# A convolution, Fourier and feed-forward kernel whose instruction order comes from a planner: other priorities, other slacks, and a charge for the tiles of 64

## The chip, the core and the metric

The kernel runs on one core of one Trainium2 chip. The metric is device microseconds (us) from the start of an execution to its end. The kernel before took 4438.63 us (the median of three runs, 4436.33 to 4449.61 us). One further execution was recorded by the hardware profiler, and that one took 4424.09 us.

## What is computed

The input is 32 images of 56 x 56 pixels with 96 channels. Cut to what matters, the reference does this to each image (all in float32 unless said otherwise):

```
layer 0   rw = sigmoid(mean(x) @ Wr + br)                  4 weights of experts for an image
          h  = relu(bn1(x @ (rw . Wpw)))                   96 -> 384 channels
          h  = relu(bn2(depthwise 3x3 with rw . Wdw))      384 channels
          x  = bn3(h @ (rw . Wpwl)) + x                    384 -> 96
layer 1   n  = layernorm(x) over channels, on 3136 tokens
          h  = relu(bn(n @ w1.T))                          96 -> 192
          X  = fft(h) over the tokens; relu of a diagonal complex product; y = real(ifft)
          x  = x + bn(y @ w2.T)                            192 -> 96
          n  = layernorm(x)
          x  = x + W2 . relu(W1 . n + b1) + b2             operands rounded to fp8 (5 exponent bits),
                                                           96 -> 384 -> 96
```

## The kernel before, in words

**The stages.** Images go through a software pipeline; three images are in work at a time. For image b the stages, with the name of the PSUM tile by which the profile knows them (the profile leaves buffer numbers out, so ps_w1 and ps_w2 are both "ps_w"), are:

- *expansion* (L678): ps_pw, 96 to 384 channels, in two halves p = 0 and 1 of the image; ScalarE evacuates to the padded tiles hp (`expanded`, L698).
- *depthwise convolution*. Part of it is on TensorE (`convolved_tensor`, L713): nine taps as diagonal 32 x 32 products, 16 array tiles at a time. One "block" of it is 144 products in the program, 288 matmuls in the profile (a float32 product runs as two). There are three blocks for an image: two in the first half (i = 0 and 1) and one in the second; below they are the first, second and third block, ps_dw. The rest is on VectorE (`convolved_vector`, L757), eight steps of scalar_tensor_tensor for a set of columns, written to the tiles h2 ("h" in the profile).
- *projection* (L783): ps_pwl, 384 to 96, four strips s = 0 to 3; VectorE adds the shortcut into x.
- *forward* (L863), two streams by the parity of s: for each strip transposes (ps_t_a) for the moments of the norm, a small product with `spread` into the same tile, then for each group of four rows of the Fourier grid ps_w1 (tiles of 96 x 64: eight products), VectorE's four `ha`, ps_a (tiles of 64 x 64: eight products), ScalarE's `g`, and a DMA to the DRAM tile gd.
- *frequency loads* (L930): when all of image b's gd is written, the first group of frequencies (16) is loaded into the one tile g2; when TensorE has read that tile, the second group (13) is loaded into the same tile.
- *frequencies* (L944): ps_b, three kinds for each group, then the complex nonlinearity on ScalarE, VectorE and GpSimd (`nonlinearity` L963, `imaginary_parts` L1001), then `spectrum` (L1019): ps_w2, ScalarE's zo, ps_c, VectorE, DMA to the DRAM tile yd.
- *inverse* (L1064), two streams by parity: loads of a strip of x1 and of yd (tile yt), ps_d, VectorE adds, transposes ps_t_f, the norm, ps_n, and the feed-forward ps_f1 (three chunks, `hidden` L1150: ScalarE, VectorE, GpSimd) and ps_f2, then GpSimd's add and the store of the output.

Work on image 16 in layer 0 stands in the program beside forward of 15 and 16, frequencies of 15 and inverse of 14. All DMAs of the steady state are issued by SyncE, in program order.

**PSUM.** There are four tiles of two banks, tag "ps", taken in turn. A TensorE group that takes a tile therefore waits until the evacuation of the group four takings earlier is done; a depthwise block takes two.

**What sets the order.** Nothing is scheduled by hand. Every stage is a generator ("stream") that yields the engine its next step runs on, the events it needs and the buffers it takes. `Plan.run` (L206) keeps a model clock for each engine; `tick` (L162) adds a modelled cost when an instruction is issued; `run` picks among the streams that could go on the one with the smallest (earliest start, priority, ready):

```
at = max(ready, self.free[stream.engine] + self.SLACK[stream.engine])
key = (at, stream.priority, ready)
```

The start is thus the later of "inputs ready" and "engine free plus SLACK" (L147, one number for each engine), and among streams that could all start when the engine is free the lower priority number wins. `mm` (L580) charges a product by its size, divided by `share` where several array tiles run at once; the depthwise block has a fixed extra of 0.4 us (L739). The order so chosen is the order of every engine's program; the chip then runs it with semaphores, and a wrong model costs waits, not errors.

**Fillers.** When the planner sees TensorE idle between two groups, `psum` (L326) puts products of the constant dftb_s into the new tile ahead of the work (L330), one for each 0.19 us of expected idle time over 0.3 us, at most 40. They compute nothing that is used. The program before holds 794.

Of the kernel before, what the change touches and what calls it, by code (L numbers as in the profile page):

```python
# [111 lines left out]
PE, DVE, ACT, POOL, SP = "PE", "DVE", "ACT", "POOL", "SP"  # L112
# [21 lines left out]
class Plan:  # L134
# [9 lines left out]

    MARGIN = 1.07

    SLACK = {PE: 0.05, DVE: 0.3, ACT: 0.05, POOL: 1.2, SP: 0.0}  # L147

    def __init__(self, **buffers):
        self.free = dict.fromkeys((PE, DVE, ACT, POOL, SP), 0.0)  # L150
# [144 lines left out]
def kernel(  # L295
# [311 lines left out]
    def mixing():  # L607

        for b in range(NB):
            yield ACT, [("x", b)] + [("x1", b - 2, s) for s in range(NS) if b >= 2]  # L610
            pooled = mixp.tile([C, 1], F32, tag="pooled", name=f"pooled_{b}")
            A.activation(xs[b], xs[b], AF.Copy, accum_out=pooled)
            yield DVE
            pool_b = mixp.tile([C, 128], F32, tag="pool_b", name=f"pool_b_{b}", bufs=1)
            V.tensor_scalar(pool_b, ones, pooled, 1.0 / N, ALU.mult, ALU.mult)
            rw = mixp.tile([128, NE + 1], F32, tag="rw", name=f"rw_{b}")
            yield POOL
            P.memset(rw[:, NE : NE + 1], 1.0)
            yield PE, (), 1
            ps = psum(f"ps_rw_{b}")  # L620
            mm(ps[:, 0:NE], pool_b, wr_s)
            yield DVE
            V.tensor_add(rw[:, 0:NE], ps[:, 0:NE], br_s)
            plan.release()
            yield ACT
            A.activation(rw[:, 0:NE], rw[:, 0:NE], AF.Sigmoid)
            yield DVE
            wk = mixp.tile([C, M], F32, tag="wk", name=f"wk_{b}")
            V.tensor_scalar_mul(wk, wpw_s[:, 0, :], rw[:C, 0:1])
            for e in range(1, NE):  # L630
                W.behind.scalar_tensor_tensor(wk, wpw_s[:, e, :], rw[:C, e : e + 1], wk, ALU.mult, ALU.add)
            yield DVE
            by = rw.rearrange("p (k e) -> p k e", k=1)
            prod = mixp.tile([128, NMIX, NE + 1], F32, tag="prod", name=f"prod_{b}", bufs=1)
            W.tensor_mul(prod, stk_s, by.to_broadcast([128, NMIX, NE + 1]))
            small = mixp.tile([128, NMIX], F32, tag="small", name=f"small_{b}")
            V.behind.tensor_reduce(small, prod, AX.X, ALU.add)
            mixed[b] = wk
            small_of[b] = small
            plan.done("wk", b)  # L640
            for c in range(NPE):
                plan.spawn("diagonals", 7, diagonals(b, c))
            yield DVE
            wk2 = mixp.tile([128, NC3, C], F32, tag="wk2", name=f"wk2_{b}")
            V.tensor_scalar_mul(wk2, wpwl_s[:, 0], rw[:, 0:1])
            for e in range(1, NE):
                W.behind.scalar_tensor_tensor(wk2, wpwl_s[:, e], rw[:, e : e + 1], wk2, ALU.mult, ALU.add)
            yield SP

            wk2s[b] = [wk2]  # L650
            for q in range(1, G):
                wk2q = mixp.tile([128, NPE, C], F32, tag=f"wk2_{q}", name=f"wk2_{b}_{q}")
                for to, at in turned(q):
                    Q.dma_start(wk2q[to], wk2[at, 0:NPE])
                wk2s[b].append(wk2q)
            arrives(4 * 3 * 128 * NPE * C, "wk2", b)
# [56 lines left out]
    def convolved_tensor():  # L713

        for b, p, before in parts_of_all():
            for i, wave in enumerate(WAVES[p]):
                needs = [("prj", *before)] if before else []
                for c in {c for c, _ in wave}:
                    needs += [("hp", b, p, c, 0), ("hp", b, p, c, 1), ("diag", b, c)]
                yield PE, needs, 2  # L720
                ps = [psum(f"ps_dw_{b}_{p}_{i}_{u}") for u in range(2)]
                for t in range(9):
                    w, h = divmod(t, 3)
                    for q, (c, k) in enumerate(wave):
                        for g in range(G):
                            at = slice(32 * g, 32 * g + 32)
                            to = 32 * ((g + q) % G)
                            bank = 512 * (q % 2)
                            lo = BW * (k % G) + w
                            mm(  # L730
                                ps[q // 2][to : to + 32, bank : bank + TB],
                                diag[b % 2][c][at, t, :],
                                hp[c][at, lo : lo + BW, h : h + S],
                                start=(t == 0),
                                stop=(t == 8),
                                share=12.7,
                            )

                plan.tick(PE, 0.4)  # L739
                plan.done("dwt", b, p, i)  # L740
                plan.spawn("evac dw", 1, convolved(b, p, i, wave, ps))

    def convolved(b, p, i, wave, ps):
        for q, (c, k) in enumerate(wave):
# [118 lines left out]
    def forward(parity):  # L863


        for b in range(NB):
            for s in range(parity, NS, 2):
# [7 lines left out]
                for q0 in range(0, n, 4):  # L875
                    yield PE, (), 1
                    ps = psum(f"ps_w1_{b}_{s}_{q0}")
                    for q in range(4):
                        for r in range(2):

                            at = S + PB * (lo + q0 + q) + S * r - 8
                            mm(
                                ps[SP64 * r : SP64 * r + SP64, 256 * q : 256 * q + CH],
                                xpad[b % 2][:, at : at + SP64],
                                w1c,
                                share=2,
                            )
                    if q0 + 4 == n:
                        plan.done("x read", b, s)
                    yield DVE  # L890
# [14 lines left out]
                    for q in range(0, 4, 2):  # L905
                        for odd in range(2):
                            for r in range(2):
                                c = r ^ odd
                                at = slice(SP64 * r, SP64 * r + SP64)
                                to = 512 * odd + 128 * q  # L910
                                mm(
                                    ps[SP64 * c : SP64 * c + SP64, to : to + CH],
                                    dfta_s[at, lo + q0 + q + odd, :],
                                    ha[at, q + odd, :],
                                    share=3.3,
                                )
                    yield ACT
                    g = sp.tile([128, 4, CH], F32, tag=f"g{parity}", name=f"g_{b}_{s}_{q0}")
                    A.copy(
# [24 lines left out]
    def frequencies():  # L944


        n = 0
        flat = g2.rearrange("p k m -> p (k m)")
        for b in range(NB):
            for i, (k0, nk) in enumerate(GROUPS):  # L950
                for kind in range(NKIND):
                    yield PE, [("g2 here", n)] + [("z read", n - 1)] * (n >= 1 and kind == 2), 1
                    ps = psum(f"ps_b_{b}_{k0}_{kind}")
                    size = (nk + (kind < 2)) // 2
                    for j in range(size):
                        at = 2 * CH * j + 128 * kind
                        mm(ps[:, 128 * j : 128 * j + PB], flat[:, at : at + 128], dftb_s)
                    plan.spawn("nonlinearity", 3, nonlinearity(n, b, k0, size, kind, ps))
                plan.done("g2", n)
                plan.spawn("spectrum", 3, spectrum(n, b, i, k0, nk))  # L960
                n += 1

    def nonlinearity(n, b, k0, nk, kind, ps):  # L963
# [12 lines left out]
        if k0 == 0 and kind < 2:  # L976
# [3 lines left out]
            V.tensor_add(u[:n0, 0, 0:1], u[:n0, 0, 0:1], dc[:n0, kind, 0:1])  # L980
            V.tensor_add(w[:n0, 0, 0:1], w[:n0, 0, 0:1], dc[:n0, kind, 1:2])
            yield ACT
            plan.spawn("imaginary parts", 5, imaginary)
        else:
            plan.spawn("imaginary parts", 2, imaginary)
            A.activation(u, re, AF.Identity, scale=rd, bias=rb)


# [75 lines left out]
    def inverse(parity):  # L1064


        for b in range(NB):
            for s in range(parity, NS, 2):
# [47 lines left out]
                for c in range(NC3):  # L1116
                    yield PE, (), 1
                    ps = psum(f"ps_f1_{b}_{s}_{c}")
                    for j in range(2):
# [2 lines left out]
                            fw1[:, 128 * c : 128 * c + 128],  # L1122
                            n[:, j * TH : j * TH + TH],
                        )
                    plan.spawn("hidden", 1, hidden(parity, b, s, c, ps, h8))
                yield PE, [("h8", b, s, c) for c in range(NC3)], 1
                ps = psum(f"ps_f2_{b}_{s}")
                for c in range(NC3):
# [34 lines left out]

    with tc.manual_schedule():
        for name, priority, stream in (
            ("loads", 2, loads()), ("mixing", 5, mixing()), ("inverse", 6, inverse(0)),
            ("inverse", 0, inverse(1)), ("frequency loads", 4, frequency_loads()),
            ("frequencies", 6, frequencies()), ("forward", 0, forward(0)),
            ("forward", 1, forward(1)), ("projection", 8, projection()),
            ("vector", 6, convolved_vector()), ("tensor", 2, convolved_tensor()),  # L1170
            ("expansion", 9, expansion()),
        ):
            plan.spawn(name, priority, stream)
        plan.run()
# [114 lines left out]
```

## Time and profile before

| What | Value |
|---|---|
| median of three runs | 4438.63 us |
| the profiled execution, its own time | 4424.09 us |
| its span, first to last instruction | 4422.3 us |
| busy: TensorE matmul, VectorE, ScalarE, GpSimd | 94%, 77%, 61%, 22% |
| granted TensorE clock, mean | 0.994 |
| first block ps_dw of image 0 starts at | 64.5 us |
| first block ps_dw of image 31 starts at | 4136.1 us |
| from one image's first block to the next one's, images 4 to 26 | 133.7 us on average |

The profiled execution was 14.5 us faster than the median of the runs. "PE" is TensorE's matmuls, "PEld" its weight loads, "DVE" VectorE, "ACT" ScalarE, "POOL" GpSimd, "SP" SyncE. In a view of waits a line reads: the engine and the tile that waited, the instruction that ended the wait, us in total, how often, the longest. "issue" is a wait that ended with no semaphore that the profile shows. In a timeline a line reads: start, duration, engine, source line, operation, tiles, shape, count, and in brackets the idle time before it and what ended it. The source line L291 is the helper that records instructions of VectorE, ScalarE, GpSimd and SyncE, and L587 is the helper that records products, so rows are told apart by their tiles.

### The profile page before, as it was taken

How to read it: one execution, taken by the hardware profiler on the slowest of the kernel's cores; microseconds unless marked ns; L12 is line 12 of the kernel's file. 1: busy time of each engine (PE TensorE's matmuls, PEld its weight loads, DVE VectorE, ACT ScalarE, POOL GpSimd, SP SyncE). 2: the span in 40 equal slices, each digit the busy share in tenths (PEclk: the TensorE clock that was granted, in tenths of full speed). 3: DMA queues.
4: the chain of work that ended last, by engine and by line, in shares of the span. 5: the costliest groups of instructions: out<-in, count | busy, mean ns of one | idle time of the engine just before them, and what ended most of it. 6: DMA issues, size and time to landing. Idle time of an engine off the chain costs nothing.

```text
span 4422.3 us, 121145 instructions
## 1 busy us (share of the span) xinstructions
PE 4160.7 (94%) x51578; PEld 2841.8 (64%) x51578; DVE 3385.6 (77%) x7256; ACT 2697.5 (61%) x4360; POOL 968.2 (22%) x1015
## 2 busy tenths in 40 slices
PE   6999999999999999999999999999999999999999
PEld 4666666666666566666666666666666666665678
DVE  6777877777878778777778887778777778787774
ACT  3465566665676666676655675655666656665565
POOL 2012222212222212222112222122222122222123
PEclk9999999999999999999999999999999999999999
DMA  3333343433344333344333434332434333444342
GB/s 87 85 93 101 78 114 95 104 94 90 91 108 105 98 96 89 96 102 108 99 98 79 106 98 109 93 103 75 114 95 107 91 97 89 104 105 100 81 107 60
DMA packets 336048, 424.96 MB, mean 96 GB/s; under 512 B 134928, under 2 KB 254544, under 8 KB 332208
## 3 DMA queue, kind: packets, MB, share of 16 engines
q1 hardware_dynamic: 333172, 417.00, 37.1%
q8 instruction: 406, 6.65, 0.7%
q14 instruction: 134, 1.10, 0.1%
q10 hardware_dynamic: 2336, 0.20, 0.0%
HBM read 202.60 MB, written 205.06 MB: 92 GB/s over the span
## 4 chain that ended last, share of the span: by engine, by line
PE 78%; DVE 7%; DMA 6%; ACT 5%; issue 3%; SPq 1%; ACTq 0%; POOL 0%; POOLq 0%; DVEq 0%
PE ps_dw L587 20%; PE ps_w L587 11%; PE ps_pw L587 10%; PE ps_pwl L587 9%; PE ps_b L587 6%; PE ps_f L587 5%; PE ps_c L587 3%; DMA yt<-yd 3%; PE ps_d L587 3%; PE ps_a L587 3%; ACT h L291 3%; PE ps_t_f L591 2%; DMA yd<-zo 2%; DVE ha L291 2%; PE ps_pw L330 1%
## 5 line engine op out<-in xcount | busy, mean ns | idle before, releaser
L291 DVE SCALAR_TENSOR_TENSOR h<-hp,small,h 128x1792 f32<-128x1792 f32 (+2 forms) x768 | 1315.0, 1712 | 20.5 <-ACT h L291 7.6
L587 PE MATMUL ps_dw<-hp,diag 32*32 32x448 f32 x27648 | 886.0, 552 | 70.0 <-issue 69.4
L587 PEld LDWEIGHTS ps_dw<-hp,diag 32*32 32x32 f32 x27648 | 531.3, 103 | 360.9 <-issue 194.1
L291 POOL CAST h<-h 128x784 fp8e5<-128x784 f16 x384 | 367.3, 970 | 1431.5 <-DVE h L291 1431.5
L587 PE MATMUL ps_pw<-x,wk 96*128 96x448 f32 (+1 forms) x1344 | 585.4, 568 | 19.8 <-ACT yt L291 19.8
L291 ACT ACTIVATE h<-ps_dw,small 128x448 f32<-128x448 f32 x384 | 225.2, 633 | 617.5 <-PE ps_dw L587 617.5
L587 PE MATMUL ps_pwl<-h,wk 128*96 128x448 f32 x1344 | 525.8, 539 | 0.0
L291 ACT ACTIVATE nl<-ps_b,nl_s 128x448 f32<-128x448 f32 (+2 forms) x576 | 347.4, 661 | 150.2 <-PE ps_b L587 86.9
L291 ACT ACTIVATE hp<-ps_pw,small 128x896 f32<-128x896 f32 (+2 forms) x384 | 355.9, 956 | 121.2 <-PE ps_pw L587 121.1
L291 POOL TENSOR_TENSOR x<-x,y 96x784 f32<-96x784 f32 x128 | 291.4, 2277 | 582.1 <-DVE y L291 578.5
L291 POOL TENSOR_TENSOR nl<-nl,nl 128x448 f32<-128x448 f32 (+1 forms) x192 | 221.9, 1156 | 757.1 <-ACT nl L291 743.0
L291 DVE SCALAR_TENSOR_TENSOR ha<-ps_w,rstd_a,nshift 128x192 f32<-128x192 f32 x896 | 307.9, 407 | 94.1 <-PE ps_w L587 93.8
L587 PEld LDWEIGHTS ps_pwl<-h,wk 128*96 128x96 f32 x1344 | 216.4, 163 | 252.2 <-issue 242.3
L587 PEld LDWEIGHTS ps_pw<-x,wk 96*128 96x128 f32 x1344 | 238.0, 190 | 210.7 <-issue 169.2
L587 PEld LDWEIGHTS ps_w<-w_s,z 128*112 128x112 f32 (+1 forms) x2816 | 351.5, 177 | 26.7 <-issue 20.5
L587 PE MATMUL ps_w<-w_s,z 128*112 128x96 f32 (+2 forms) x2816 | 367.0, 284 | 0.0
L291 ACT ACTIVATE nt<-yt,nm,rstd_f 112x96 fp8e5<-112x96 f32 x896 | 334.2, 454 | 41.3 <-DVE nm L291 41.3
L587 PE MATMUL ps_b<-dftb_s,g 112*128 112x112 f32 x2816 | 351.8, 277 | 7.4 <-DMA g<-gd 4.6
L587 PEld LDWEIGHTS ps_b<-dftb_s,g 112*128 112x128 f32 x2816 | 335.5, 193 | 27.8 <-ACT h L291 10.4
L587 PE MATMUL ps_w<-w1c,x 96*64 96x192 f32 x3584 | 334.0, 332 | 7.7 <-ACT h L291 7.0
L291 DVE TENSOR_SCALAR h<-h,fb 128x784 f16<-128x784 f16 x384 | 229.9, 613 | 140.4 <-ACT h L291 137.9
L291 ACT CAST h<-ps_f 128x784 f16<-128x784 f32 x384 | 294.4, 822 | 49.1 <-PE ps_f L587 44.7
(163 smaller groups left out, 5737.3 us busy)
## 6 DMA issues: line engine op xcount, KB each, us to landing
gd<-g SPq DMA_DIRECT2D x448, 192.0 KB
g<-gd SPq DMA_DIRECT2D x64, 672.0 KB
x<-in_x_dram SPq DMA_DIRECT2D x32, 1176.0 KB
x<-x SPq DMA_DIRECT2D x128, 294.0 KB
yt<-yd SPq DMA_DIRECT2D x128, 294.0 KB
out_dram<-x SPq DMA_DIRECT2D x128, 294.0 KB
g<-gd SPq DMA_DIRECT2D x64, 546.0 KB
x<-x SPq DMA_DIRECT2D x96, 336.0 KB
```

What stands on the lines that cost most here:

```text
L291: return getattr(self.namespace, name)(out, *args, **kw)
L330: nc.tensor.matmul(ps[:PB, 0:PB], dftb_s, dftb_s, start=True, stop=True)
L587: nc.tensor.matmul(to, lhsT, rhs, start=start, stop=stop)
L591: nc.tensor.transpose(to, ap, eye)
```

## The change

The operations of the computation stay what they are. Changed are the numbers by which the planner orders them: two engines' slacks, the priorities of most streams, and two new charges on the model clock of TensorE, 0.1 us after each group of ps_w1 and 0.16 us after each group of ps_a.

```diff
-    SLACK = {PE: 0.05, DVE: 0.3, ACT: 0.05, POOL: 1.2, SP: 0.0}
+    SLACK = {PE: 0.05, DVE: 0.2, ACT: 0.1, POOL: 1.2, SP: 0.0}
...
-                plan.spawn("diagonals", 7, diagonals(b, c))
+                plan.spawn("diagonals", 6, diagonals(b, c))
...
-                plan.spawn("evac dw", 1, convolved(b, p, i, wave, ps))
+                plan.spawn("evac dw", 5, convolved(b, p, i, wave, ps))
...
                                 share=2,
                             )
+                    plan.tick(PE, 0.1)
                     if q0 + 4 == n:
                         plan.done("x read", b, s)
                     yield DVE
...
                                     share=3.3,
                                 )
+                    plan.tick(PE, 0.16)
                     yield ACT
...
-                    plan.spawn("nonlinearity", 3, nonlinearity(n, b, k0, size, kind, ps))
+                    plan.spawn("nonlinearity", 2, nonlinearity(n, b, k0, size, kind, ps))
...
-            plan.spawn("imaginary parts", 5, imaginary)
+            plan.spawn("imaginary parts", 3, imaginary)
         else:
-            plan.spawn("imaginary parts", 2, imaginary)
+            plan.spawn("imaginary parts", 4, imaginary)
...
-                    plan.spawn("hidden", 1, hidden(parity, b, s, c, ps, h8))
+                    plan.spawn("hidden", 0, hidden(parity, b, s, c, ps, h8))
...
-            ("loads", 2, loads()), ("mixing", 5, mixing()), ("inverse", 6, inverse(0)),
-            ("inverse", 0, inverse(1)), ("frequency loads", 4, frequency_loads()),
-            ("frequencies", 6, frequencies()), ("forward", 0, forward(0)),
-            ("forward", 1, forward(1)), ("projection", 8, projection()),
-            ("vector", 6, convolved_vector()), ("tensor", 2, convolved_tensor()),
+            ("loads", 6, loads()), ("mixing", 1, mixing()), ("inverse", 3, inverse(0)),
+            ("inverse", 7, inverse(1)), ("frequency loads", 1, frequency_loads()),
+            ("frequencies", 7, frequencies()), ("forward", 5, forward(0)),
+            ("forward", 3, forward(1)), ("projection", 9, projection()),
+            ("vector", 8, convolved_vector()), ("tensor", 6, convolved_tensor()),
             ("expansion", 9, expansion()),
```

Both programs were built and their orders laid side by side. From about the fourth image on each repeats one pattern for every image. This is TensorE's pattern in the part of an image around the third depthwise block, in the numbers of image 16 (names are tile, image, then strip, group or chunk):

```
before  ... pw_16_1_1_1, pwl_16_1, t_a_16_0 spread, d_14_3, t_a_16_1, n_14_0, b_15_0_0, t_f_14_3,
        w1_16_0_0, t_a_16_1 spread, f1_14_0_0, f1_14_0_1, a_16_0_0, f1_14_0_2, b_15_0_1, w1_16_0_4,
        w1_16_1_0, a_16_0_4, n_14_3, a_16_1_0, f2_14_0, f1_14_3_0..2, w1_16_1_4, b_15_0_2,
        dw_16_1 (third block), f2_14_3, a_16_1_4, w2_15_0_0, b_15_16_0, c_15_0_0, ...
after   ... pw_16_1_1_1, pwl_16_1, d_14_2, t_a_16_0 spread, b_15_0_0, n_14_1, t_a_16_1, t_f_14_2,
        f1_14_1_0, f1_14_1_1, t_a_16_1 spread, f1_14_1_2, b_15_0_1,
        dw_16_1 (third block), w1_16_1_0, n_14_2, w1_16_0_0, f1_14_2_0..2, a_16_1_0, f2_14_1,
        a_16_0_0, b_15_0_2, w1_16_1_4, f2_14_2, w1_16_0_4, a_16_1_4, fillers, w2_15_0_0, a_16_0_4,
        b_15_16_0, c_15_0_0, d_14_3, ...
```

In both programs SyncE's second load of g2 waits for b_15_0_2, and ps_b of the second group (b_15_16_0) waits for that load. The program after holds 752 fillers, 42 fewer; all other counts of products are the same.

## The prediction

> **What bounds the kernel now.** I read the page first, then TensorE's waits, then the timelines of TensorE and SyncE around the costliest one.
>
> ```profile
> span 4422.3 us, 121145 instructions
> PE 4160.7 (94%) x51578; PEld 2841.8 (64%) x51578; DVE 3385.6 (77%) x7256; ACT 2697.5 (61%) x4360; POOL 968.2 (22%) x1015
> q8 instruction: 406, 6.65, 0.7%
> ```
>
> TensorE is busy 94% of the span, so it is the bound; the other three have room. What the order can change is TensorE's idle time, 262 us, of which 37 us is one wait before the first image. The view of TensorE's waits splits the rest (us in total, times, longest):
>
> ```profile
> PE ps_dw L587 <- issue: 69.4, 38, 3.9
> PE ps_a L587 <- DVE ha L291: 24.2, 29, 0.8
> PE ps_d L587 <- DMA yt<-yd: 23.0, 23, 1.9
> PE ps_pw L587 <- ACT yt L291: 19.8, 30, 0.7
> PE ps_t_f L591 <- DVE x L291: 18.6, 30, 0.7
> PE ps_a L587 <- ACT h L291: 12.8, 30, 0.4
> PE ps_n L587 <- DVE nl L291: 12.2, 29, 0.4
> ```
>
> All but the first and third come 29 or 30 times, once an image: they are places in the repeating order. The largest is inside the depthwise block, and no semaphore ended it. TensorE's timeline of one image (start, duration), then SyncE's, then the DMA view of 2071.3 to 2078.8 us and of 2078.8 to 2081 us:
>
> ```profile
> 2069.71 2.04 PE L587 MATMUL ps_b<-dftb_s,g 112*128 112x112 f32 x16
> 2071.68 6.89 PE L587 MATMUL ps_dw<-hp,diag 32*32 32x448 f32 x224
> 2081.73 2.13 PE L587 MATMUL ps_dw<-hp,diag 32*32 32x448 f32 x64 [3.16 <-issue]
> ```
> ```profile
> 2071.33 0.87 SPq L291 DMA_DIRECT2D g<-gd  x2
> ```
> ```profile
> q1 hardware_dynamic: 1455, 1.10, 78.1%
> ```
> ```profile
> q1 hardware_dynamic: 29, 0.01, 4.5%
> q8 instruction: 1, 0.02, 3.9%
> ```
>
> The third block begins at 2071.68, just after b_15_0_2 has freed g2 and SyncE has issued the second load of g2 (2071.33). While that load runs (its packets span 2072.3 to 2079.2) the queue of instructions moves nothing; its packet starts at 2078.9, as the load ends, and TensorE goes on at 2081.7. 406 packets for 51578 matmuls are one for 127 matmuls. A block starts a matmul every 29 ns and uses 127 in 3.7 us, half the load's 7 us. From first to last start an undisturbed block takes 8.3 us. By that measure (it counts the pipeline's last half us, which the waits leave out) the 32 third blocks lose 94.5 us, the first blocks 13.7 and the second ones 1.3.
>
> [...] 6.65 MB in 406 packets, 254 weight loads and matmuls each. [...] here the instruction packet came only when the load ended. [...] beyond the usual step from start to start, a change costs 0.25 us out of tiles of 64 (ps_w1, ps_a), 0.45 us out of 32, 0.09 us out of the rest.
>
> **The change part by part.** *TensorE's own work.* Counted in the built orders, the products are the same, so their time (counts by the trace's steps from start to start) stays. Passages out of tiles of 64 rise from 354 to 379: 25 x 0.25 = +6 us. Fillers fall from 794 to 752: 42 x 0.2 = -8 us at most, less where they covered idle time. Passages and fillers counted in, both orders come to 125.0 us an image in the repeating part, and an image takes 133.7. The charge of the model buys nothing by itself; what counts is what becomes of the 8.7 us of waits.
>
> *The third block moves ahead of b_15_0_2*: it starts 57 us into an image's work instead of 72, and the load that stalled it is triggered 9 us after its end. During the load's 8 us TensorE then runs ps_w1, ps_f2, ps_a and ps_w2, some 130 matmuls in 9.5 us. In the block above 131 matmuls ran between the point where the packet was due (127 after the last one) and the stall, so the instructions in hand last the load out. Around its new place SyncE has only two stores of x1 and six small copies of wk2. I take the loss of the third blocks from 94.5 to 5 us: **-90**. Bounds: 0 and -94.5.
>
> *The first block* lost 13.7 us beside the loads of x1 and yt, issued 1 to 2 us after its start. They now stand about 3 us earlier: **-5**, between -13 and +10.
>
> *Waits outside the blocks*, from start to start (the view above leaves out the pipeline's end, so these are larger). Before they come to 6.05 us an image over 27 images: ps_a behind ha 1.15, ps_d behind yt 0.94, ps_pw behind yt 0.86, ps_t_f behind x 0.79, ps_a behind h 0.50, ps_n behind ha 0.49, a filler behind h 0.40, ps_w1 behind h 0.30, eight small ones 0.62. For both orders I measured each wait's lead: the TensorE work between the group that feeds an evacuation and the group that waits. Where the lead is short of the evacuations queued plus about 0.3 us for the semaphores (ps_pw: lead 0.20, yt 0.72, waited 0.86) the rest is the wait.
> - Gone: ps_w1 to ps_a had leads of 1.2 and 1.3 against four ha of 0.41; it now has 2.0 or more. ps_pw behind yt, ps_n behind ha and ps_w1 behind h go with their neighbours. A filler stays at 0.4, ps_a behind h at 0.35, ps_t_f (leads 3.0 to 4.5 where they were 2.8 to 3.3) at 0.5.
> - ps_d behind yt: the chain is x's load (6.2 us), gd's writes, g2's load (landed 11.7 us after x's), then yt. It passes one store of x1 (1.6 us) that stood before it, but the first of these ps_d stands 1.4 us earlier. I take 0.5.
> - New: f1_14_0_2 behind ha_15_2_4 (lead 1.55, need 1.7) 0.4. In the stretch b_15_0_0 to b_15_0_1 ScalarE has seven evacuations of 0.6 to 0.8 us for PSUM queued (nl, n8, yt, h16): f1_14_1_0 0.7, f1_14_1_1 (lead 0.34 behind yt) 1.1, b_15_0_1 0.6, and the spread product of t_a_16_1 (lead 1.31, VectorE's statistics 2.7, of which 1.8 have then been waited) 0.1. That of t_a_16_2 (lead 2.26) 0.7. w2_15_0_0 behind z 0.25. x of strip 1, now behind wk2 (1.6 us) on VectorE: 0.3. The second load of g2 (8 us) had 13.8 us of work to cover it and has 9.2, with a write of gd ahead: b_15_16_0 0.5, d_14_3 0.2.
>
> Sum after: 0.4 + 0.35 + 0.5 + 0.5 + 0.4 + 0.7 + 1.1 + 0.6 + 0.1 + 0.7 + 0.25 + 0.3 + 0.5 + 0.2 = 6.6 us, 0.55 more, over 29 images **+16**.[...] Each lead is known to some half a microsecond, and VectorE's and ScalarE's backlog isn't shown for an order that hasn't run: 4.5 to 9 us, -45 to +86.
>
> *What is late next.* GpSimd's casts keep leads of 5 us. VectorE worked on in the 3 us of each stall and loses them, but its 106 us of busy time fit in 131. *Head and tail*: 29 fillers fewer in the head, 15 more in the tail: **-2**.
>
> Sum: -90 - 5 + 16 - 2 = -81 us. From the profiled execution's 4424.1 that is 4343; the median of the runs stood 14.5 us above that execution, so **4358 us**.
>
> **The rivals.** A: as above, with 5.6 to 7.8 us of other waits: 4328 to 4392. B: the short waits shrink as well, to 4.5 us an image: -81 - 61 = -142, 4297. For it: the new leads of ps_a are long everywhere; against it: seven leads under 2.3 us are new. C: the stall in the block turns into a wait of ps_b and ps_d for the same load, now with the short cover: 2.5 us more an image, +73, 4431, no change. For it: that load and yt queue on the same engines; against: TensorE's other new waits lengthen the cover. D: the fetch stall moves along with the block, as other packets take the load's place: +90 instead of -90's gain, 4448. Against it: second blocks, beside little traffic, lose 1.3 us in all. E, on the other side: VectorE runs late. One more convolution step (1.71 us) ahead of three of the new short leads (spread of t_a_16_1, spread of t_a_16_2, f1_14_0_2) is 5.1 us an image, +149, 4507. It decides from 3.3 us an image above today's 6.05, where it eats the 97 us of the blocks. For it: VectorE is the second busiest engine, and its slack in the planner falls from 0.3 to 0.2. Against: the statistics stand at the head of its order there.
>
> **How the numbers follow.** A 0.55, B 0.15, C 0.10, D 0.06, E 0.14. A 0.3% change is 13 us, about what a measurement can tell from none: below 4425 is faster, above 4452 slower. A, B and a fifth of C are faster: 0.72; the rest of C, most of D: 0.13; E and the edge of D: 0.15. The range 4290 to 4450 holds A, C, D and most of B, some 0.8.
>
> **What would show it.** In the profile after: ps_dw behind issue under 15 us instead of 69.4; ps_a behind ha nearly gone; new rows of about 20 us each for ps_f behind ScalarE's yt and ps_t_a behind dm_a; the image's period near 131 us. The forecast is wrong if ps_dw behind issue stays, if ps_b or ps_d behind a DMA passes 60 us, or if TensorE's waits for VectorE grow beyond 100 us.

## The result, and the profile after

The kernel after took **4368.01 us** (median of four runs, 4362.64 to 4377.89); the kernel before, on the same chip, 4444.12 us (the three runs named above and a fourth, 4451.40 us). The ratio is 0.9832, 95% interval 0.9804 to 0.9859. The forecast was 4358 us, faster. The profiled execution of after took 4369.82 us, 54 us less than that of before, while the medians differ by 76: the profiled execution of before lay 20 us below its median here, that of after 1.8 above.

The page and TensorE's waits in the profile of after:

```profile
span 4368.0 us, 121017 instructions
PE 4186.2 (96%) x51494; PEld 2864.5 (66%) x51494; DVE 3351.6 (77%) x7256; ACT 2724.9 (62%) x4360; POOL 961.3 (22%) x1015
q8 instruction: 405, 6.64, 0.6%
```
```profile
PE ps_d L587 <- DMA yt<-yd: 38.4, 26, 2.3
...
PE ps_f L587 <- ACT yt L291: 18.2, 29, 0.6
PE ps_t_a L587 <- DVE dm_a L291: 16.6, 31, 0.7
PE ps_f L587 <- ACT n L291: 14.7, 27, 0.5
PE ps_b L587 <- DMA g<-gd: 7.8, 14, 1.4
...
PE ps_a L587 <- ACT h L291: 4.5, 19, 0.3
PE ps_dw L587 <- issue: 2.6, 5, 1.1
...
PE ps_t_f L591 <- DVE x L291: 0.9, 2, 0.5
```

The stall in the depthwise blocks is gone (ps_dw behind issue, 69.4 to 2.6 us), as are ps_a behind ha (24.2) and ps_pw behind yt (19.8). The new rows are those that were forecast, and ps_d behind yt has grown from 23.0 to 38.4. But compare the first lines: the operations of the computation are the same, there are 84 matmuls fewer (the 42 fillers, two matmuls each), and TensorE is busy 25 us *longer* (4160.7 before). The same work then takes TensorE longer. TensorE's timeline of one image shows where (columns as before, the idle time ahead of a row in brackets):

```profile
2025.02 0.74 PE L591 MATMUL ps_t_f<-ident,x 96*112 96x96 f32 x7
2026.30 0.49 PE L587 MATMUL ps_f<-n,fw 96*128 96x392 fp8e5 x2 [0.55 <-ACT n L291]
2027.43 0.49 PE L587 MATMUL ps_f<-n,fw 96*128 96x392 fp8e5 x2 [0.64 <-ACT yt L291]
2028.47 0.50 PE L587 MATMUL ps_t_a<-dm_a,spread 112*128 112x8 f32 x2 [0.54 <-DVE dm_a L291]
2028.82 0.81 PE L587 MATMUL ps_f<-n,fw 96*128 96x392 fp8e5 x2
2029.43 3.59 PE L587 MATMUL ps_b<-dftb_s,g 112*128 112x112 f32 x16
2032.95 9.91 PE L587 MATMUL ps_dw<-hp,diag 32*32 32x448 f32 x288
```

The same 16 matmuls of ps_b took 2.04 us in the timeline of before; here they take 3.59, and the block takes 9.91 us instead of the 8.8 of an undisturbed one. Nothing waits in these rows. The view by stretches (PE's busy time in the second column, the granted clock behind POOL's) has the reason:

```profile
core 0: us, PE busy (x) PEld busy (x) DVE busy (x) ACT busy (x) POOL busy (x), PEclk, DMA share, GB/s
2022.00:2025.60 3.60, 3.60 (x42) 3.60 (x41) 1.79 (x3) 1.66 (x4) 0.00 (x0) 1.00 0.14 34
2025.60:2029.00 3.40, 1.68 (x9) 0.76 (x8) 3.33 (x15) 3.23 (x5) 1.13 (x1) 0.94 0.52 144
2029.00:2032.40 3.40, 3.40 (x17) 3.30 (x15) 3.19 (x6) 1.91 (x4) 2.28 (x3) 0.50 0.04 14
```

After a stretch with 1.68 us of work in 3.40, the granted clock is 0.50, and ps_b and the block run in it. The records of the granted clock show such stretches, of 3.41 or 6.83 us, 14 times before (26.8 us lost: the length times the part not granted) and 22 times after (54.6 us). Of the 22, 18 begin 1.8 to 5 us ahead of a third block, right behind these short waits, three 10 to 14 us ahead of one, and one in the tail. The mean clock on the page hides it: 0.994 before, 0.988 after.

The block's own place worked out as planned. SyncE's timeline of after for the image whose third block ran from 2032.95 to 2042.8:

```profile
2052.47 1.18 SPq L291 DMA_DIRECT2D g<-gd  x2
```

The second load of g2 is now issued 10 us after the block's end.

**Where the time went, per image.** To have a sum that closes, I split the 24 images from the first block of image 4 to that of image 28 into the steps from each matmul's start to the next one's. The period fell from 133.71 to 132.55 us, by 1.16:

| Part of an image | before, us | after, us | change |
|---|---|---|---|
| steps inside the three blocks ps_dw | 28.45 | 25.65 | -2.80 |
| steps inside ps_b (half clock) | 9.32 | 10.44 | +1.12 |
| all the rest: other tiles, passages, waits | 95.94 | 96.46 | +0.52 |

These 24 images hold 28 of the 54 us that separate the two profiled executions. Of the rest, 7.5 lie ahead of image 4's first block, 12 in the periods of images 28 to 30, and 7 behind the first block of image 31. Split in the same way, the whole run has -85 us in the blocks, +28 in ps_b and +3 in all the rest.

### The profile page after: what moved, and what is told of

It is laid out like the page before. It is cut to its first block, busy times and chain, and to the rows that moved or that the text cites. A ratio compares the mean times of both kernels' runs of the same rounds, so it can differ in the third digit from the quotient of the medians.

```text
span 4368.0 us, 121017 instructions
## 1 busy us (share of the span) xinstructions
PE 4186.2 (96%) x51494; PEld 2864.5 (66%) x51494; DVE 3351.6 (77%) x7256; ACT 2724.9 (62%) x4360; POOL 961.3 (22%) x1015
## 3 DMA queue, kind: packets, MB, share of 16 engines
q14 instruction: 133, 1.09, 0.1%
## 4 chain that ended last, share of the span: by engine, by line
PE 75%; DMA 10%; DVE 8%; ACT 5%; issue 1%; SPq 1%; POOL 1%; ACTq 0%; POOLq 0%
PE ps_dw L587 17%; PE ps_w L587 13%; PE ps_pw L587 10%; PE ps_b L587 7%; PE ps_pwl L587 6%; DMA yt<-yd 6%; PE ps_d L587 4%; PE ps_f L587 4%; PE ps_a L587 4%; PE ps_c L587 4%; DMA g<-gd 3%; DVE h L291 2%; DVE ha L291 1%; ACT x L291 1%; ACT h L291 1%
## 5 line engine op out<-in xcount | busy, mean ns | idle before, releaser
L291 DVE SCALAR_TENSOR_TENSOR h<-hp,small,h 128x1792 f32<-128x1792 f32 (+2 forms) x768 | 1259.3, 1640 | 54.4 <-ACT h L291 40.6
L587 PE MATMUL ps_dw<-hp,diag 32*32 32x448 f32 x27648 | 865.9, 550 | 3.7 <-issue 2.6
L291 POOL CAST h<-h 128x784 fp8e5<-128x784 f16 x384 | 413.0, 1099 | 1593.5 <-DVE h L291 1593.2
L587 PEld LDWEIGHTS ps_dw<-hp,diag 32*32 32x32 f32 x27648 | 540.2, 104 | 267.4 <-issue 100.6
L587 PE MATMUL ps_b<-dftb_s,g 112*128 112x112 f32 x2816 | 381.8, 292 | 15.6 <-DMA g<-gd 7.8
L587 PEld LDWEIGHTS ps_b<-dftb_s,g 112*128 112x128 f32 x2816 | 360.2, 206 | 39.0 <-issue 14.6
L291 POOL TENSOR_TENSOR nl<-nl,nl 128x448 f32<-128x448 f32 (+1 forms) x192 | 210.2, 1095 | 695.3 <-ACT nl L291 694.5
L291 POOL TENSOR_TENSOR x<-x,y 96x784 f32<-96x784 f32 x128 | 243.6, 1903 | 398.2 <-DVE y L291 395.3
L587 PEld LDWEIGHTS ps_w<-w1c,x 96*64 96x64 f32 x3584 | 237.8, 136 | 76.0 <-issue 25.9
```

Source lines behind the costliest of these rows:

```text
L291: return getattr(self.namespace, name)(out, *args, **kw)
L587: nc.tensor.matmul(to, lhsT, rhs, start=start, stop=stop)
```

## The experiments

All times are device microseconds. Each set of runs has its own runs of before beside it (medians 4434 to 4444), so kernels of different sets are compared by their ratios to before; the last column turns the difference of ratios into us at 4440. By the two intervals such a difference is known to some 15 us. before_short_load and after_short_x leave out part of a load, and with it part of the computation.

| Kernel | median | ratio to before, 95% interval | half clock: stretches, us lost | us against after |
|---|---|---|---|---|
| after | 4368.01 | 0.9832 (0.9804 to 0.9859) | 22, 54.6 | 0 |
| before_short_load | 4332.61 | 0.9762 (0.9746 to 0.9777) | 4, 14.7 | -31 |
| charges_only | 4594.37 | 1.0358 (1.0335 to 1.0382) | 31, 123.0 | +234 |
| orders_only | 4419.53 | 0.9965 (0.9952 to 0.9977) | 20, 46.6 | +59 |
| after_fillers | 4337.73 | 0.9775 (0.9760 to 0.9790) | 6, 16.4 | -25 |
| before_long_packets | 4386.81 | 0.9893 (0.9876 to 0.9909) | 8, 19.8 | +27 |
| fillers_elsewhere | 4400.29 | 0.9915 (0.9894 to 0.9935) | 25, 54.7 | +37 |
| after_short_x | 4302.23 | 0.9700 (0.9685 to 0.9714) | 16, 34.9 | -59 |
| fillers_long_packets | 4293.90 | 0.9680 (0.9664 to 0.9695) | 3, 8.5 | -67 |
| after_long_packets | 4328.12 | 0.9747 (0.9719 to 0.9775) | 24, 59.4 | -38 |
| three_fillers | 4333.42 | 0.9773 (0.9751 to 0.9795) | 6, 18.4 | -26 |

**1. Is it the load that stalls the block?** The order of before, with the second load of g2 cut short.

```diff
+                few = 3 if i else nk
-                        g2[S * c : S * c + S, 0:nk, :],
+                        g2[S * c : S * c + S, 0:few, :],
```

> The kernel before in its own order, but the second load of g2 fetches 3 of its 13 frequencies (the other ten keep what the first load left, so that part of the spectrum is not the input's). Theory: the third depthwise block stalls because this load keeps the instruction packets waiting. The load then takes under 2 us instead of 7, a block outlasts that, and ps_dw behind issue falls from 69.4 us to under 15; the third blocks' loss falls from 94.5 us to under 20, and the half-clock windows that follow the stalls go too (12 before the drain): 75 to 105 us faster than before. Rival: the stall belongs to the block, which uses instructions faster than they can come, whatever else moves; then it stays above 50 us and the time falls by under 20 us.

It ran 105 us faster than before, at the upper edge of what the theory gave. TensorE's longest waits in its profile (but for the one ahead of the first image), and that of the blocks:

```profile
PE ps_d L587 <- DMA yt<-yd: 25.3, 24, 2.1
PE ps_a L587 <- DVE ha L291: 24.2, 29, 0.8
PE ps_pw L587 <- ACT yt L291: 19.8, 30, 0.7
...
PE ps_dw L587 <- issue: 5.4, 10, 1.0
```

The other waits are nearly where they were in before (ps_d behind yt 25.3 us instead of 23.0). Only ps_dw behind issue has gone, from 69.4 to 5.4 us, and the third blocks' loss from 94.5 to 1.2. So the load causes the stall: the order and all else were left as they were. That the gain exceeds the 93 us of the blocks fits the clock: 11 of the 14 half-clock stretches in before begin 8.8 to 11.5 us after the start of a third block that lost 2.6 to 6.2 us, and the loss in such stretches falls by 12 us. Without its stall, and with part of a load left out, the order of before is 31 us faster than the kernel after.

**2. What do the two charges do, and what the new priorities and slacks?** Before with the two charges alone; after without them.

```diff
+                    plan.tick(PE, 0.1)
+                    plan.tick(PE, 0.16)
```

> The kernel before with the two charges alone (0.1 us after ps_w1, 0.16 us after ps_a), old slacks and priorities. Built, its order is another one: 1214 fillers instead of 794, 417 passages out of tiles of 64 instead of 354, and 134.9 us of work and fillers an image instead of 125.0; the second load of g2 is triggered 6.7 us ahead of the third block, so that only its last 1.5 us lie beside it. Theory (the gain comes from where the third block stands and which waits are left, not from a truer model): the fillers lie partly in real idle time; blocks lose under 25 us instead of 94.5; in all 20 us faster to 120 us slower than before, most likely some 40 us slower. Rival: the truer model is what counts: 30 us or more faster than before.

> The kernel after without the two charges: its slacks and priorities alone. Built, its pattern is that of after around the third block (57.3 us into an image's work, ahead of b_15_0_2), with few groups exchanged later, but 1056 fillers instead of 752, nine more of them an image ahead of w2_15_0_0: 127.0 us of work and fillers an image instead of 125.0. Theory: it keeps the gain of the blocks (third blocks lose under 20 us) and pays for fillers where TensorE isn't idle: 20 to 55 us slower than after (4368), so 20 to 55 us faster than before. Rival: without the charges the gain goes: within 15 us of before or slower.

The charges alone made before 3.6% slower, more than I had allowed for: a miss. The page of that run:

```profile
PE 4339.8 (95%) x52418; PEld 2990.5 (65%) x52418; DVE 3369.2 (73%) x7256; ACT 2709.8 (59%) x4360; POOL 1050.0 (23%) x1015
```

TensorE's own work goes up: with the old priorities the charged model finds an order with 1214 fillers instead of 794 and an image of 134.9 us of products, passages and fillers instead of 125.0, and its profile has 31 stretches at half clock. The new priorities and slacks without the charges take the block's stall away too:

```profile
PE ps_dw L587 <- issue: 2.3, 2, 2.1
```

But they are 59 us slower than after, near the upper end of the theory's 20 to 55: this order holds 1056 fillers, 304 more than after, and the steps inside fillers ahead of ps_w2 take 2.51 us an image instead of 0.58. So the stall goes with the new priorities and slacks, but most of the gain in time needs the charges as well: without them 16 us are left of 75. By the account of steps the charges matter for the fillers that they keep out; no run took out those fillers alone. That a truer cost of passages (0.25 us out of tiles of 64 in the trace of before) pays as such isn't shown: with the old priorities it made the kernel slower. Priorities and slacks weren't run apart.

**3. Is it the half clock that ate the rest?** Eight unused products an image in after, at the three short waits: two behind ps_t_f of strip 2, three behind the first ps_f1 of strip 1, and three narrow ones ahead of the spread product of strip 1. Then, as a control, the same eight behind the last projection, where TensorE waits for nothing.

```diff
+    def fill(ps, at, width, count):
+        for _ in range(count):
+            nc.tensor.matmul(ps[:PB, at : at + width], dftb_s, dftb_s[:, 0:width], start=True, stop=True)
...
+        if who == "f0" and lo == 0 and name.endswith("_2"):
+            fill(ps, 896, 112, 2)
...
+            if who == "a1" and name.endswith("_1"):
+                fill(ps, 224, 32, 3)
...
+                    if (s, c) == (1, 0):
+                        fill(ps, TH, PB, 3)
```

> The kernel after in its own order, with eight unused products added an image where TensorE waits ahead of the third block: two behind ps_t_f of strip 2, three behind the first ps_f1 of strip 1, three ahead of the spread product of strip 1. Theory: the half-clock windows of the kernel after (20 of them before the drain, just ahead of the third block, some 50 us lost) come from this stretch of short waits; with TensorE kept at work they become fewer than eight, ps_b's busy time falls from 382 to near 352 us, and the time falls by 15 to 40 us against after (4368), to about 4340. Rival one: only the waits count, the fillers cover them and cost nothing: within 8 us of after, windows as before. Rival two: the fillers come in the way of the products behind them: 8 x 0.2 x 29 = 46 us, less the 50 us of waits they may cover: up to 20 us slower than after.

> The kernel after with the same eight unused products an image as the run with fillers in the waits, but all eight behind the last projection (ps_pwl of strip 3), where TensorE waits for nothing. My theory (they help where they stand in the stretch of short waits, because the clock is kept up and their own time is hidden in the waits): some 20 windows at half clock stay, 45 to 60 us lost in them, and the eight products cost up to their own 1.4 us an image: 15 to 45 us slower than the kernel after. The rival (what helps is a small delay anywhere in the image, against the loads): as fast as with the fillers in the waits, 20 to 35 us faster than the kernel after.

In the waits, the added work made the kernel 25 us *faster*; 6 stretches at half clock are left of 22, none of them within 10 us ahead of a third block, and the steps inside ps_b fall from 10.44 to 9.63 us an image. Behind the projection it cost 37 us, 25 stretches stayed, and each image holds the added products in full (1.41 us; its period is 0.75 us longer, since other waits shrank). That is as the theory had it. The rival (a delay anywhere) is out for this place, the only other one tried. The next run asks how little is enough:

> The kernel after with only the three unused products ahead of the spread product of strip 1 (three of the eight, 0.6 us). My theory[...]: one of three waits filled takes away some of the windows, 8 to 16 are left, and the time is 8 to 25 us under the kernel after. The rival (any one of the waits left is enough): 18 to 22 windows, within 8 us of the kernel after.

(That text misplaces the three products: they are the three behind the first ps_f1 of strip 1, the last part of the diff above.) They are 0.75 us of work, and in time they do as much as the eight: 26 us faster, 6 stretches, just over the 8 to 25 us and fewer than the 8 to 16 stretches that I had given. In the timeline of that run they fill the middle one of the three waits, and the outer two stay as they were:

```profile
2016.63 0.49 PE L587 MATMUL ps_f<-n,fw 96*128 96x392 fp8e5 x2 [0.55 <-ACT n L291]
2016.96 0.75 PE L591 MATMUL ps_f<-dftb_s 112*112 112x112 f32 x6
2017.76 0.49 PE L587 MATMUL ps_f<-n,fw 96*128 96x392 fp8e5 x2
2018.80 0.39 PE L587 MATMUL ps_t_a<-dm_a,spread 112*128 112x8 f32 x2 [0.54 <-DVE dm_a L291]
2019.04 0.49 PE L587 MATMUL ps_f<-n,fw 96*128 96x392 fp8e5 x2
2019.39 2.04 PE L587 MATMUL ps_b<-dftb_s,g 112*128 112x112 f32 x16
2021.36 8.80 PE L587 MATMUL ps_dw<-hp,diag 32*32 32x448 f32 x288
```

ps_b is back at 2.04 us and the block at 8.80, with 1.1 us of waiting ahead of them instead of 1.7.

**4. What is ps_d waiting for?** After, with x's load cut to a quarter of each image.

```diff
+            few = N // 4 if b > 2 else N
-                Q.dma_start(xs[b], x[b])
+                Q.dma_start(xs[b][:, 0:few], x[b][:, 0:few])
```

> The kernel after, whose load of x fetches a quarter of each image from the fourth on (the rest of x is left over from an earlier image; order and all other work stay). My theory (the 38 us in which ps_d waits for yt end a chain that starts with x's load of 6 us on the same queues): ps_d behind yt falls below 15 us and the time by 15 to 40 us. The rival (that chain is set by g2's load or the writes of yd): ps_d behind yt stays above 28 us and the time within 10 us.

TensorE's waits in that run, to set against 38.4 and 7.8 in after:

```profile
PE ps_b L587 <- DMA g<-gd: 6.4, 10, 1.3
...
PE ps_d L587 <- DMA yt<-yd: 2.8, 5, 1.1
```

ps_d's wait is gone with the bytes of x, so x's load is a link of that chain without which it ends in time. It isn't the only one: experiment 5 takes 22 us off the same wait with x's load whole. In the profile of after one queue, q1, moves 417.0 of the 424.9 MB; the loads of x, of g2 and of yt have over 35 MB each, so they stand in it together, and from 2052.5 to 2060 us, where loads of g2 and yt are issued, its packets take 96.4% of the time of 16 engines. The time fell by 59 us where 15 to 40 were forecast: beside ps_d's passages (2.52 to 1.09 us an image) those of ps_f fell by 0.60 and ps_b's steps by 0.50, the latter with six stretches at half clock fewer.

**5. Fewer packets.** With the axes of the DRAM tile gd turned, a row's frequencies lie side by side: the loads of g2 move packets of 12,288 and 9,984 bytes instead of 768, and the writes of g packets of 768 instead of 3,072. Nothing is left out. I ran it in before, in after, and in after with the eight fillers.

```diff
-                    gds[b] = dram.tile([2, SP64, NQ, CH], F32, tag="gd", name=f"gd_{b}")
+                    gds[b] = dram.tile([2, NQ, 2, SP64 // 2, CH], F32, tag="gd", name=f"gd_{b}")
...
-                    for c in range(2):
-                        Q.dma_start(gd[c, :, at : at + 4, :], g[SP64 * c : SP64 * c + SP64])
+                    for i in range(2):
+                        Q.dma_start(gd[i, at : at + 4].rearrange("q c k m -> (c k) q m"), g[i::2])
...
-                        gds[b][c, 2 * k0 : 2 * (k0 + nk)].rearrange("(k i) q m -> (i q) k m", i=2),
+                        gds[b][:, :, c, k0 : k0 + nk].rearrange("i q k m -> (i q) k m"),
```

> The kernel before with its own order and all of its computation; only the DRAM tile gd has its axes turned, so that the loads of g2 find the frequencies of a row side by side (packets of 12,288 and 9,984 bytes instead of 768) and the writes of g leave in packets of 768 bytes instead of 3,072. My theory (the many small packets of the second load of g2 keep the instruction packet out for 7 us): the load is over in 3 to 4 us, the 127 matmuls in hand last 3.7 us, so ps_dw behind issue falls from 69 us to under 25 and the time by 60 to 105 us. The rival (it is the bytes that hold the queues, or the trigger of the load, whatever its packets): ps_dw behind issue stays above 50 and the time stays within 20 us; the four times as many packets of the writes may even cost 10 to 20.

> The kernel after with the eight unused products in the waits and with gd's axes turned (all of the computation). My theory: the block is no longer at stake, but the two loads of g2 land 3 us sooner, so ps_d behind yt (36 us with the fillers) falls to 10 to 20 and ps_b behind the load goes: 15 to 35 us faster than with the fillers alone, 4300 to 4325 us. The rival (the writes' fourfold packets hold the same queues as long as the loads gain): within 10 us of the fillers alone, ps_d's wait unchanged.

> The kernel after, with gd's axes turned and no unused products added (all of the computation). Beside the fillers the turn was worth 44 us, 21 of them in ps_d behind yt. If the two causes are independent (the loads' chain here, the clock there), the time is 35 to 55 us under the kernel after (4313 to 4333), ps_d behind yt falls from 38 to about 15, and some 20 windows at half clock, 45 to 60 us lost, stay. The rival (the wait of ps_d is one of those that bring the clock down): under 12 windows, and 60 to 80 us under the kernel after.

In before the stall shrank but stayed, which misses both expectations. TensorE's timeline of one block in that run, then the DMA view of 2049.1 to 2055.2 us and of 2055.2 to 2056.6 us:

```profile
2049.47 6.45 PE L587 MATMUL ps_dw<-hp,diag 32*32 32x448 f32 x202
2057.97 2.13 PE L587 MATMUL ps_dw<-hp,diag 32*32 32x448 f32 x64 [2.05 <-issue]
```
```profile
DMA packets 132, 1.12 MB, mean 183 GB/s; under 512 B 20, under 2 KB 20, under 8 KB 20
q1 hardware_dynamic: 132, 1.12, 78.4%
```
```profile
q8 instruction: 1, 0.02, 5.7%
q1 hardware_dynamic: 8, 0.00, 0.5%
```

Over the whole run TensorE's wait in the blocks is:

```profile
PE ps_dw L587 <- issue: 46.1, 32, 3.3
```

The load moves 1.12 MB (twice the 546 KB of one issue) at 183 GB/s and lasts 6.2 us (2049.6 to 2055.8) instead of 6.9: a thirteenth of the packets made it a tenth shorter, so mostly it isn't their number that sets its length, and my 3 to 4 us were wrong. With 112 packets in place of 1456 the instruction packet of this block still starts only near the load's end (2055.2). The stall fell from 69.4 to 46.1 us, which is about what a load shorter by 0.7 us in each of some 30 images gives. The kernel ran 47 us faster than before; most of the rest is ps_d (behind yt 9.0 us instead of 23.0) and 7 us less lost at half clock.

The two blocks shown here and in the prediction are of the commoner kind. In before, 29 third blocks have a second load of g2 beside them. In 21 of them no instruction packet started until 92% of the load's packets were over, and the block lost 1.9 to 6.2 us. In the other eight one started when only 4 to 51% were over, and the block lost at most 2.3 us. The same eight images stand apart in before_long_packets (12 to 62%, against 84% and more). Why some instruction packets get in amid the load wasn't examined.

In the orders of after the turn took 38 us (alone) and 42 us (beside the fillers), ps_d behind yt going from 38.4 to 16.3 and from 36.3 to 15.0; beside the fillers 15 to 35 us had been forecast. Alone it left 24 stretches at half clock, so the loads' chain and the clock are two separate causes, as expected there. Why the chain gains more than two loads' 0.7 us explain wasn't taken apart.

fillers_long_packets, 4293.9 us, does all of the computation and beats both kernels: 3.2% faster than before, 67 us faster than after.

## Why the prediction was right, and where it was not

**The bound and the main step** held. *The third block moves ahead of b_15_0_2* was put at -90 us: the third blocks' loss fell from 94.5 to 14.0, -80. The 14 that are left are hardly that stall (ps_dw behind issue is 2.6 us): with the clock kept up by the fillers they are 1.4. Experiment 1 shows the step's reason by itself. That the instruction packet comes only when the load ends was read from one block, and holds for 21 of the 29 (experiment 5).

***The first block***: -5 forecast; its loss fell from 13.7 to 8.2.

***Waits outside the blocks***: 0.55 us an image more was forecast, and the closed account gives 0.52 more for all that is neither block nor ps_b. The total came out right, its terms only in part, so that luck has a share in it: ps_d alone was 1.5 us an image off, and others by as much the other way. Gone as forecast: ps_a behind ha, ps_pw behind yt. There as forecast: ps_f behind ScalarE's yt and ps_t_a behind dm_a, 18.2 and 16.6 us, and ps_f behind n, counted with them as f1_14_1_0. Better than forecast: ps_t_f, put at 0.5 us an image, is 0.9 us in the whole run. Wrong in sign: ps_d behind yt, put at 0.44 us an image less, and by the closed account its passages cost 1.08 more (1.44 to 2.52). I had named its chain (x's load, gd, g2, yt) and let one store less in front of it outweigh an earlier ps_d; experiment 4 shows that cutting x's load takes that wait away and more.

***Sum***: the profiled execution was to be 4343 us and was 4369.8: 27 us too low. The step that failed is the one on *TensorE's own work*, which says that its "time (counts by the trace's steps from start to start) stays". The work stayed, the clock did not. Over the whole run the steps inside ps_b took 28 us more, where nothing was forecast (24 of the 28 lie in steps that began at a clock of 0.50), and the blocks gave 85 us instead of 95, mostly for the same reason. All the rest, which holds the waits outside the blocks and the head and tail, came to +3 us instead of +14 and hid 11 of these 38. The profile of before had the sign of it (14 stretches, a mean clock of 0.994), and I didn't ask whether the new row of short waits would add to them. That the median was missed by only 10 us has a second reason, and it is luck: I carried the 14.5 us between the profiled execution and the median of before over to after, where the same distance was -1.8. Two errors of opposite sign, 27 and 16, met.

**The rivals.** A held in its cause and nearly in its time. B is out as stated, since the rest didn't shrink. Of C there is a trace: ps_b and ps_d behind DMAs went from 27.6 to 46.2 us, in the direction it gave and at a quarter of its price, most of it in ps_d, whose wait hangs on x's load as well (experiment 4). D is out: the stall didn't move along. E is out: ps_t_a and ps_f behind VectorE come to 22 us. No rival had the clock in it.

## What to carry to other kernels

A long load issued beside a dense run of small matmuls cost more here (69.4 us in before) than any of the waits that repeat with the images (24.2 us and less). Look for idle time "behind issue", lay SyncE's timeline beside it, and try the same program with that one load cut short. When TensorE's busy time grows while its instructions don't (4160.7 to 4186.2 us here, with 84 matmuls fewer), read the granted clock by stretches of a few microseconds; the mean of the span hides it (0.988, with 22 stretches at 0.50). Here a few unused products in the right wait brought it back (6 stretches, 25 us faster), while the same products elsewhere only cost time (25 stretches, 37 us slower). Split the period so that the parts sum to it, since a list of waits doesn't show a slower clock: here it left out the 28 us that ps_b took more.

## What the runs showed of the hardware that I had not expected

- **The half clock without a long gap.** The stretches at 0.50 in after, 3.41 or 6.83 us long, all begin on one grid of 3.413 us. Three gaps of 0.54 to 0.64 us within 2.7 us stood ahead of 17 of the 22 and two of these gaps ahead of an 18th; with the middle gap filled (three_fillers) 6 stretches were left. Measured on that grid, in the steady part of before each step of 3.413 us at full clock in which TensorE was busy at most 0.44 of the time was followed by half clock and none above; in after, 21 that were followed by it were busy 0.40 to 0.66, beside 18 of 0.47 to 0.66 that were not. A sharp limit isn't shown, and neither is what sets the clock.
- **Beside the second load of g2 the instruction packet mostly came as the load ended, with many packets or few.** In 21 of 29 images of before none started until 92% of the load's packets were over. In the two blocks shown, with 1456 or with 112 packets for the same 1.12 MB, the one instruction packet of 16,384 bytes started as the load ended, 7.6 and 6.6 us after the load's issue, and the block stood for 3.16 and 2.05 us. In the other eight images of before one started when 4 to 51% of the load's packets were over, and the block lost at most 2.3 us.
